# A softmax total moved from VectorE to ScalarE in a top-p graph attention kernel

## The chip, the cores and the metric

The kernel runs on one core of a Trainium2 chip. A core has five engines with an instruction stream each: TensorE (PE, whose weight loads the profile lists apart as PEld), VectorE (DVE), ScalarE (ACT), GpSimd (POOL) and SyncE (SP, which here only starts transfers). Each engine carries out its own instructions strictly in order, and the engines wait for each other through semaphores. The metric is the device time in microseconds (us) of one execution.

## The reference: what is computed

There are 3327 nodes with 256 features each. Layer 0 is a sparse graph attention with a gated update and two layer norms. Layer 1 makes two steps of a top-p ("nucleus") attention beside a propagation over the graph, then two layer norms. The change lies in layer 1, in its second step (n = 1):

```python
for n in range(STEPS):                       # STEPS = 2
    A = _top_p_attention(Xa, W1, W2, W3)     # 3327 x 3327, row-stochastic
    Xf = R @ Xf
    Xa = A @ Xa
    Z = Z + Xf @ U1[n].T + Xa @ U2[n].T

def _top_p_attention(X, W1, W2, W3):
    logits = (X @ W1.T @ W2.T) @ (X @ W3.T).T
    probs = softmax(logits)
    # keep the largest of each row until their sum reaches TOP_P = 0.9, drop the rest
    keep_sorted = cs - sp < TOP_P            # cs: running sum of the sorted sp
    A = probs * mask
    return A / max(A.sum(-1), 1e-12)
```

So each row of exponentials needs its total: 0.9 of the total is the mark at which the kept set ends.

## The kernel before, in words

The rows of the attention are cut into NT = 26 tiles of 128 rows (the last has 127). Layer 0 and step 0 of layer 1 take the first 900 us of the execution and are not touched. Step 1 is the class `Layer1`, method `run`, from its second `with` on. The order of the instructions on PE, ACT, DVE and POOL is written out by hand there: no scheduler moves them. The loop runs over tiles i, and each pass is one call of `product(i, slots)`: PE turns the 26 column blocks of the masked exponentials of tile i in seven groups of four (`turn`, L2052, with ACT copying each turned group out of PSUM, L2054) and multiplies them with the features (`times`, L2068). Two groups are turned ahead before the first product, and behind every group of products the functions that hang in that group's slot are issued. They belong to later tiles, so that four tiles are in work at once:

- tile i+3: its logits on PE (`chunk`, L1779), copied to SBUF by ACT (L1782), in slots 0 to 3;
- tile i+2: its candidates, the eight largest of each of 32 column groups, on DVE (`eights`, L1795) and minus the row's largest (`highest`, L1870) in slot 1; the exponentials of the candidates (`exp_candidates`, L1890) and of the first half of the row (`exp`, L1878) in slot 3, of the second half in slot 4. These are ACT's. Each half writes the sum of its own 1664 or 1663 exponentials into one column of a small tile `sums`; the trace shows this as an ACTIVATION_READ_ACCUMULATOR behind each half;
- tile i+1: `list_1` on DVE, issued ahead of slot 0: it takes the candidates' exponentials, tries four cut values (L1904, four passes with a sum each), makes `thr2` = 2 x 0.9 x (sum of the two halves) (L1907), compares the four sums with it (L1909), and sorts what is left; then in slot 1 `list_2` finds the smallest kept exponential, and in slot 3 `mask` (L1982, L1948) writes the masked row, which the next pass turns;
- tile i-1 and older: the layer norms, on ACT and POOL (`sums`, L2031 to L2043).

`thr2` is column 2 of a tile of four columns called `pay` (L1869), which has four buffers. Later readers of `thr2` are `settle` (L1829, DVE), `one_over` (L1958, POOL) and the transfer `put_aside_2` (L2140, POOL), which writes `pay` away for rows that the fast path cannot finish. Those rows are treated in a tail ("hard" rows, L2147 to L2313) behind the last tile; some of that work, L2207 and L2225 on ACT, lies between the last eight tiles.

At the start of a pass ACT's order is: second half's exponentials of tile i+1 (as counted from the new i) and their read-out (L1878), `h` of the tile just multiplied (`scaled`, L2076), and then the copy of the first turned group (L2054), for which PE waits before its first product. The prediction calls this place the handover.

Of the kernel before, what the change touches and what calls it, by code (L numbers as in the profile page):

```python
# [11 lines left out]
AF = mybir.ActivationFunctionType  # L12
ALU = mybir.AluOpType
# [13 lines left out]
TOP_P = 0.9  # L27
# [1221 lines left out]
class Layer1:  # L1249
# [91 lines left out]
    def parts_0(self, t):  # L1341
# [136 lines left out]
        def exp(k):  # L1478
# [3 lines left out]
            nc.scalar.activation(signs[:r, on], l[:r, on], AF.Exp, bias=v.nmax[:r], accum_out=v.sums[:r, k : k + 1])  # L1482

        parts["exp0"], parts["exp1"] = lambda: exp(0), lambda: exp(1)

        @part
# [387 lines left out]
    def exp(self, i, h):  # L1874

        v = self.items[i]
        on = slice(h * HALF, min(N, (h + 1) * HALF))
        self.nc.scalar.activation(  # L1878
            v.p[: v.r, on], v.l[: v.r, on], AF.Exp, bias=v.nmax[: v.r], accum_out=v.sums[: v.r, h : h + 1]
        )  # L1880

    def exp_candidates(self, i):

        v = self.items[i]
        width = -(-N // GROUP[v.n]) * 8
        if i == NT:
            v.ec = self.work.tile([P, 2 * D], F32, tag="xt", name=f"ec{v.tag}", bufs=3)[:, :width]
        else:
            v.ec = self.work.tile([P, width], F32, tag="xtq", name=f"ec{v.tag}")
        self.nc.scalar.activation(v.ec[: v.r], v.cand[: v.r], AF.Exp, bias=v.nmax[: v.r])  # L1890

    def list_1(self, i):

        nc, v = self.nc, self.items[i]
        r, tag, ec = v.r, v.tag, v.ec
        by_rank = ec[:r].rearrange("p (g e) -> p e g", e=8)
        first, end = TRIED
        tried = end - first
        high = self.small("high", f"high{tag}", tried)
        nc.vector.tensor_reduce(high[:r], by_rank[:, first:end, :], AX.X, ALU.max)  # L1900
        v.last = self.last_eights(ec, r, tag)
        above = self.small("upto", f"above{tag}", tried)
        for j in range(tried):
            nc.vector.scalar_tensor_tensor(  # L1904
                v.cand[:r], ec[:r], high[:r, j : j + 1], ec[:r], ALU.is_ge, ALU.mult, accum_out=above[:r, j : j + 1]
            )
        nc.vector.tensor_scalar(v.thr2[:r], v.sums[:r, 0:1], v.sums[:r, 1:2], 2.0 * TOP_P, ALU.add, ALU.mult)  # L1907
        over = self.small("at", f"over{tag}", tried)
        nc.vector.tensor_scalar(over[:r], above[:r], 2.0, v.thr2[:r], ALU.mult, ALU.is_ge)  # L1909
        v.e = self.work.tile([P, LIST[1] + 1], F32, tag="e", name=f"e{tag}")  # L1910
        v.lst = v.e[:, 1:]
        skip = self.small("u", f"skip{tag}")
        nc.vector.scalar_tensor_tensor(high[:r], over[:r], 2.0, high[:r], ALU.mult, ALU.max)
        nc.vector.tensor_reduce(skip[:r], high[:r], AX.X, ALU.min)
        nc.vector.scalar_tensor_tensor(v.cand[:r], ec[:r], skip[:r], ec[:r], ALU.is_lt, ALU.mult)
        nc.vector.scalar_tensor_tensor(above[:r], over[:r], 0.5, above[:r], ALU.is_lt, ALU.mult)
        nc.vector.tensor_reduce(v.e[:r, 0:1], above[:r], AX.X, ALU.max)
        for _ in self.sort(v.cand, r, LIST[1], tag, v.lst):
            pass
# [733 lines left out]
```

## Time and profile before

| what | value |
|---|---|
| median of 3 runs (lowest, highest) | 1627.8 us (1625.9, 1630.64) |
| profiled execution: its own time, its span | 1629.77 us, 1628.0 us |
| TensorE clock granted, mean over the span | 0.93 |
| busy over the span: PE, DVE, ACT, POOL | 87%, 84%, 68%, 64% |
| stage 0 to 880 us: layer 0 and step 0 | PE 780.6, DVE 700.9, ACT 644.5, POOL 517.2 us busy |
| stage 920 to 1440 us: most of step 1's tiles | PE 500.0, DVE 495.2, ACT 356.6, POOL 418.5 us busy |
| stage 1480 to 1628 us: the tail with the hard rows | PE 66.1, DVE 111.9, ACT 54.7, POOL 60.5 us busy |

How to read it: the time is that of a separate counter, the span is what the instructions of the profile cover; the two differ by 1.8 us. In a row of the timeline the first number is the start in us from the span's start, the second the duration, then engine, line, operation, what is written and read, and in brackets the idle time before and who ended it. Several neighbouring instructions of one line are merged (x8); fp32 matmuls appear as two passes each. A busy engine is not by that the one that sets the time: that is read from who waits for whom in the stage in question. The transposes' "weights" are the masked row, so that PE cannot begin them before DVE has masked it.

### The profile page before, as it was taken

How to read it: one execution, taken by the hardware profiler on the slowest of the kernel's cores; microseconds unless marked ns; L12 is line 12 of the kernel's file. 1: busy time of each engine (PE TensorE's matmuls, PEld its weight loads, DVE VectorE, ACT ScalarE, POOL GpSimd, SP SyncE). 2: the span in 40 equal slices, each digit the busy share in tenths (PEclk: the TensorE clock that was granted, in tenths of full speed). 3: DMA queues.
4: the chain of work that ended last, by engine and by line, in shares of the span. 5: the costliest groups of instructions: out<-in, count | busy, mean ns of one | idle time of the engine just before them, and what ended most of it. 6: DMA issues, size and time to landing. Idle time of an engine off the chain costs nothing. (4 is left out here: it accounts for less than half of the span.)

```text
span 1628.0 us, 27192 instructions
## 1 busy us (share of the span) xinstructions
PE 1414.7 (87%) x7743; PEld 967.2 (59%) x7743; DVE 1372.0 (84%) x4921; ACT 1103.1 (68%) x2690; POOL 1036.4 (64%) x1484
## 2 busy tenths in 40 slices
PE   4899999986899899998988899999999999988334
PEld 3756666554455555555555477777777666666233
DVE  5799999537888888888874899999999998987984
ACT  4478888755688878888774567676666777773730
POOL 0366666514566766767654378888888878877440
PEclk7599999996799999999999799999999999999667
DMA  8978776314334444444443112222222222121000
GB/s 261 329 248 261 261 256 178 83 40 123 95 113 117 124 127 111 123 118 128 124 113 85 38 49 68 72 72 75 66 75 58 75 62 75 54 59 33 26 13 5
DMA packets 101636, 178.80 MB, mean 110 GB/s; under 512 B 25975, under 2 KB 64118, under 8 KB 101478
## 3 DMA queue, kind: packets, MB, share of 16 engines
q0 software_dynamic: 26288, 73.75, 17.5%
q1 hardware_dynamic: 61818, 93.49, 17.4%
q10 hardware_dynamic: 13372, 9.76, 1.9%
q8 instruction: 63, 1.03, 0.3%
q14 instruction: 95, 0.78, 0.2%
HBM read 139.92 MB, written 37.07 MB: 109 GB/s over the span
## 5 line engine op out<-in xcount | busy, mean ns | idle before, releaser
L2068 PE MATMUL pav<-xu,at 128*128 128x256 f32 (+2 forms) x1352 | 339.1, 396 | 20.4 <-ACT at L2054 20.4
L2068 PEld LDWEIGHTS pav<-xu,at 128*128 128x128 f32 (+2 forms) x1352 | 249.2, 194 | 113.4 <-issue 44.6
L1782 ACT COPY array<-pl 128x416 f32<-128x416 f32 (+3 forms) x402 | 184.3, 512 | 125.9 <-PE pl L1779 125.6
L1795 DVE MAX8 cand<-array 128x8 f32<-128x104 f32 (+5 forms) x1233 | 260.5, 288 | 7.0 <-ACT array L1782 6.8
L1779 PE MATMUL pl<-kT,qT 64*128 64x416 f32 (+3 forms) x804 | 205.7, 570 | 9.2 <-ACT array L1782 8.0
L2054 ACT COPY at<-pt 128x512 f32<-128x512 f32 (+2 forms) x182 | 95.4, 539 | 106.3 <-PE pt L2052 106.0
L677 POOL DMA_INDIRECT g<-x_rows,edge x130 | 136.9, 1053 | 45.0 <-issue 30.3
L677 POOL DMA_INDIRECT g<-whx,edge x130 | 134.9, 1038 | 46.9 <-issue 37.2
L677 POOL DMA_INDIRECT g<-y_rows,edge x130 | 136.6, 1051 | 36.9 <-issue 35.6
L1608 POOL DMA_INDIRECT g<-x1k,uidx x130 | 136.6, 1051 | 36.8 <-issue 25.7
L945 DVE FIND_INDEX8 at<-ones,array 128x8 uint32<-128x840 f32 (+1 forms) x104 | 105.9, 1027 | 0.0
L1779 PEld LDWEIGHTS pl<-kT,qT 64*128 64x128 f32 (+1 forms) x804 | 66.8, 188 | 65.8 <-issue 44.3
L1705 POOL TENSOR_TENSOR x<-x,c 128x256 f32<-128x256 f32 (+1 forms) x26 | 17.7, 684 | 73.5 <-ACT c L1700 73.5
L1062 PE MATMUL acc<-g,m 128*128 128x258 f32 (+1 forms) x260 | 62.7, 388 | 0.0
L2011 PE MATMUL pxf<-g,m 128*128 128x256 f32 (+1 forms) x260 | 62.4, 387 | 0.0
L1062 PEld LDWEIGHTS acc<-g,m 128*128 128x128 f32 (+1 forms) x260 | 50.5, 195 | 18.4 <-issue 7.4
L1666 PE MATMUL pav<-g,w 128*128 128x257 f32 (+1 forms) x260 | 60.9, 380 | 0.0
L2085 POOL TENSOR_TENSOR h<-h 128x256 f32<-128x256 f32 (+1 forms) x26 | 58.7, 2257 | 2.0
L1904 DVE SCALAR_TENSOR_TENSOR cand<-ec,high 128x256 f32<-128x256 f32 (+1 forms) x104 | 57.0, 548 | 2.8
L1089 PE MATMUL prz<-wih,hT 128*128 128x512 f32 (+1 forms) x104 | 52.1, 625 | 3.5 <-ACT hT L1082 1.6
L701 PE MATMUL pq<-xtq,wkqk 128*128 128x128 f32 (+1 forms) x208 | 35.5, 295 | 21.5 <-ACT xtq L693 15.4
L701 PEld LDWEIGHTS pq<-xtq,wkqk 128*128 128x128 f32 x208 | 29.9, 195 | 39.3 <-ACT xtq L693 38.1
(578 smaller groups left out, 3809.9 us busy)
## 6 DMA issues: line engine op xcount, KB each, us to landing
array<-in_adj_dram SPq DMA_DIRECT2D x25, 1248.0 KB
array<-in_adj_dram SPq DMA_DIRECT2D x25, 415.5 KB
members<-m SPq DMA_DIRECT2D x26, 320.0 KB
m<-members SPq DMA_DIRECT2D x26, 320.0 KB
x_rows<-x ACTq DMA_DIRECT2D x25, 128.0 KB
x1k<-x ACTq DMA_DIRECT2D x25, 128.0 KB
xb_rows<-xb SPq DMA_DIRECT2D x25, 128.0 KB
y_rows<-y SPq DMA_DIRECT2D x25, 128.0 KB
```

Of the source, the lines that this page charges most:

```text
L677: self.nc.gpsimd.indirect_dma_start(out=dst[:, b, :], out_offset=None, in_=table[:, :], in_offset=bass.IndirectOffsetOnAxis(ap=self.edge[: ...
L701: nc.tensor.matmul(pq[:, :r], self.wkqk[:, c, h * DA : h * DA + P], xt[:, c, :r], start=(c == 0), stop=(c == DC - 1))
L945: nc.vector.max_index(at[:r, g, :], self.ones8[:r], ad[:r, g, :])
L1062: nc.tensor.matmul(acc[:r, : self.WH], m[:, :r], g[:, k, :], start=(k == 0), stop=(k == EB - 1))
L1608: nc.gpsimd.indirect_dma_start(out=v.g2[:, b, :], out_offset=None, in_=sh.x1k[:, :], in_offset=bass.IndirectOffsetOnAxis(ap=v.idx[:, b : b ...
L1666: nc.tensor.matmul(v.acc[:r, : D + 1], v.w[:, b, :r], v.g2[:, b, : D + 1], start=(b == 0), stop=(b == UB - 1))
L1779: nc.tensor.matmul(pl[:r, :w], q[on], self.sh.kT[on, n, s : s + w], start=True, stop=True)
L1782: nc.scalar.copy(l[:r, h * HALF + s : h * HALF + s + w], pl[:r, :w])
L1795: self.nc.vector.max(cand[:r, g * 8 : g * 8 + 8], src[:r, g * group : min(N, (g + 1) * group)])
L2011: nc.tensor.matmul(acc[:r, :D], v.m[:, b, :r], v.g[:, b, :], start=(b == 0), stop=False)
L2054: nc.scalar.copy(at[:, :full, :r], pt[:, :full, :r])
L2068: nc.tensor.matmul(v.acc[: v.r, :D], at[:k, j - 4 * g, : v.r], V[:k, j, :], start=(j == 0), stop=(j == NT - 1))
```

## The change

`thr2` is no longer made on DVE in `list_1`. ACT makes it right behind the second half's exponentials, with two instructions on 128x1 operands: the first half's sum is scaled in place by 2 x 0.9, and the second half's sum is scaled by the same factor and added to it, the first serving as per-partition bias. `list_1` loses one instruction.

```diff
@@ def exp(self, i, h):
         self.nc.scalar.activation(
             v.p[: v.r, on], v.l[: v.r, on], AF.Exp, bias=v.nmax[: v.r], accum_out=v.sums[: v.r, h : h + 1]
         )
+        if h:
+            a, b = v.sums[: v.r, 0:1], v.sums[: v.r, 1:2]
+            self.nc.scalar.activation(a, a, AF.Copy, scale=2.0 * TOP_P)
+            self.nc.scalar.activation(v.thr2[: v.r], b, AF.Identity, bias=a, scale=2.0 * TOP_P)
@@ def list_1(self, i):
-        nc.vector.tensor_scalar(v.thr2[:r], v.sums[:r, 0:1], v.sums[:r, 1:2], 2.0 * TOP_P, ALU.add, ALU.mult)
         over = self.small("at", f"over{tag}", tried)
         nc.vector.tensor_scalar(over[:r], above[:r], 2.0, v.thr2[:r], ALU.mult, ALU.is_ge)
```

In the built program this adds 52 instructions to ACT (two for each of 26 tiles), each waiting for the ACT instruction before it, and takes 26 from DVE. The order on PE, POOL and SP is the same as before, and ACT and DVE keep the order of all else. The comparison L1909 waits for ACT's second new instruction, where L1907 used to wait for the read-out. In 22 of the 26 tiles the second new instruction also waits for the transfer that last read its buffer of `pay`, four tiles earlier. Behind the change, lines of the file shift by 4 (up to L1907 of before) or 3.

## The prediction

> **What bounds the kernel now.** I read the stage that holds the change first: the busy time by stretch, then who waits for whom in it.
>
> ```profile
> core 0: us, PE busy (x) PEld busy (x) DVE busy (x) ACT busy (x) POOL busy (x), PEclk, DMA share, GB/s
> 920.00:1440.00 520.00, 499.95 (x2493) 370.24 (x2492) 495.21 (x1640) 356.57 (x810) 418.54 (x694) 0.99 0.23 67
> ```
> ```profile
> PE pav L2068 <- ACT at L2054: 13.1, 22, 1.9
> ...
> DVE pay L1907 <- ACT array L1878: 0.8, 1, 0.8
> ```
>
> PE (96%) and DVE (95%) are both nearly full, ACT is at 69%. That would favour taking work from DVE. But PE's largest wait is for ACT: 22 times, once a tile, for the copy at the handover (columns: us in total, times, longest). DVE waits almost not at all. So the handovers have to be read one by one in the timeline. There are three kinds. The first, at 966 us:
>
> ```profile
> 966.07 1.07 PE L2052 MATMUL pt<-ident,array 128*128 128x128 f32 x8
> 967.44 1.78 PE L2068 MATMUL pav<-xu,at 128*128 128x256 f32 x7 [0.29 <-ACT at L2054]
> ...
> 966.23 0.21 ACT L1878 ACTIVATION_READ_ACCUMULATOR p<-array,pay 128x1 f32 x1
> 966.33 0.49 ACT L2076 ACTIVATE h<-pav,rA 128x256 f32<-128x256 f32 x1
> 966.80 1.07 ACT L2054 COPY at<-pt 128x512 f32<-128x512 f32 x2
> ```
>
> The copy begins 0.73 us after the transposes; PE's first product always follows the copy's start by 0.64 to 0.66. The copy stands 0.47 behind L2076; where nothing holds it, that distance is 0.36 (third kind, below). So ACT has 0.11 us to spare. Here DVE is not in the way (the mask ended at 964.91): PE runs at its own pace, from 944.37 over 966.07 to 987.77, 21.70 a tile. The second kind, from 1009.65 to 1206.85, ten handovers:
>
> ```profile
> 1075.18 0.08 DVE L1948 DVE_READ_ACCUMULATOR p<-p,t 128x1 f32 x1
> ...
> 1075.41 1.06 PE L2052 MATMUL pt<-ident,p 128*128 128x128 f32 x8
> ...
> 1075.32 0.21 ACT L1878 ACTIVATION_READ_ACCUMULATOR array<-array,pay 128x1 f32 x1
> 1075.41 0.49 ACT L2076 ACTIVATE h<-pav,rA 128x256 f32<-128x256 f32 x1
> 1076.13 1.07 ACT L2054 COPY at<-pt 128x512 f32<-128x512 f32 x2 [0.23 <-PE pt L2052]
> ```
>
> Each time the transposes start 0.15 to 0.16 after the mask's end: DVE sets the pace, (1206.85 - 1009.65) / 9 = 21.91 a tile, only 0.21 above PE's own. ACT's spare is 0.28 to 0.36. The third kind, 1345.95 to 1415.74, where hard-row work (L2225) lies on ACT too:
>
> ```profile
> 1371.14 0.48 ACT L2076 ACTIVATE h<-pav,rA 128x256 f32<-128x256 f32 x1
> 1371.49 1.09 ACT L2054 COPY at<-pt 128x512 f32<-128x512 f32 x2
> ...
> 1372.15 1.99 PE L2068 MATMUL pav<-xu,at 128*128 128x256 f32 x8 [1.86 <-ACT at L2054]
> ```
>
> ACT never stops before the copy and PE stands still for 1.86 us: no spare at all.
>
> **What is removed.** One L1907 in each of 26 tiles on DVE.
>
> ```profile
> 1076.58 0.08 DVE L1904 DVE_READ_ACCUMULATOR cand<-ec,high 128x1 f32 x1
> 1076.70 0.49 DVE L1904 SCALAR_TENSOR_TENSOR cand<-ec,high 128x256 f32<-128x256 f32 x1
> ...
> 1077.64 0.08 DVE L1904 DVE_READ_ACCUMULATOR cand<-ec,high 128x1 f32 x1
> 1077.64 0.21 DVE L1907 TENSOR_SCALAR pay<-sums 128x1 f32<-128x1 f32 x1
> 1077.88 0.23 DVE L1909 TENSOR_SCALAR over<-above,pay 128x4 f32<-128x4 f32 x1
> ```
>
> L1907 overlaps the read-out. L1909 needs the read-out itself, and what depends on one starts 0.12 behind its start (1076.58 to 1076.70): it moves from 1077.88 to 1077.76. So DVE gains 0.12 a tile, not 0.24: its pace where it leads would be 21.79. Where L1909 already follows ACT, nothing is gained.
>
> **What is added.** Two dependent ACT instructions, between the read-out (start A) and L2076. The nearest rows:
>
> ```profile
> L2037 ACT ACTIVATE junk2bt<-h,minbt 128x256 f32<-128x256 f32 x21 | 10.9, 521 | 0.0
> ...
> L2031 ACT ACTIVATE junkbt<-h 128x256 f32<-128x256 f32 x21 | 9.0, 430 | 0.0
> ...
> L2033 ACT ACTIVATE minat<-sat 128x1 f32<-128x1 f32 x22 | 4.5, 203 | 0.7
> ```
>
> (Columns: busy us, mean ns, idle before.) L2033 is the very Copy (128x1, 203 ns, behind a read-out). The Identity has a pointer bias besides: L2037 has one and L2031 none, 521 - 430 = 91 ns, so about 295 ns (an estimate). L2033 starts 0.22 behind the read-out's start (1060.36 to 1060.58). The Copy then starts at A + 0.22, the Identity a Copy and a gap of 0.03 later at A + 0.455, and L2076, which need not wait for it, about 0.2 on at A + 0.655, against A + 0.09 now: ACT's handover is 0.56 us later.
>
> Here a rule of the Trainium skill decides (ScalarE: Activation LUTs, section "What ACT_TABLE_LOAD costs"): an ACTIVATE has some 186 ns of fixed cost, each pointer operand adds about 93, and instructions back to back overlap by about 93. The 91 ns agree. By the overlap the two would cost 0.09 + 0.19 = 0.28, all but hidden by the spare of the second kind, and the total would be about +1 us. But the overlap is that of independent instructions (read-out to L2076: 0.09); the dependent row shows 0.22. I take 0.56; 0.28 is the lower end, and 0.7 the upper if either semaphore costs a little more. No new function is used (Exp, Copy and Identity alternate now), so I add no table load. The wait for the transfer out of `pay` costs nothing: L1870 on DVE wrote that buffer after the same landing, and the exponentials read it.
>
> Queued behind on ACT: L2076, whose reader on POOL (L2077, at 1081.23) has over 5 us; and the copy L2054, for which PE waits, with all its later work in order behind. From the first product on PE has no idle time in a tile of the first two kinds, so a delay there is not made up within the tile.
>
> On the DVE side, where L1909 waits for ACT it moves from read-out end + 0.28 to about + 0.58: +0.30. Six tiles wait so now (906, 1324, 1347, 1370, 1443, 1467 us); elsewhere the slack is up to 2.2 us. DVE then still masks more than 1 us ahead of PE.
>
> **The sum.**
> - Start: the first pair of exponentials (906 us) stands before copies on the chain to the first handover: +0.5.
> - 944 to 1207: the delay is 0.56 - 0.11 = 0.45, PE's pace 22.15, above DVE's 21.79. Twelve tiles: 12 x 22.15 = 265.8 against 262.5: +3.3. The gain on DVE is lost in this, since PE now sets the pace.
> - 1229 and 1251: 0.45 each; 1274: 0.2, as L2076 waits for POOL there anyway; 1299 and 1324: 0.35 each (spare 0.21): +1.8.
> - Given back: PE's wait of 0.8 for POOL's flag at 1212 and some 0.9 for a gather at 1281 (0.4 idle, 0.5 stretched) lie on DVE's and POOL's chain, which is not delayed as much: -1.7.
> - 1346 to 1416: four with no spare, +2.2; 1466: +0.6. At 1442 ACT waits 2 us for POOL: 0.
> - The last tile's L1909 lies on the chain into the tail: +0.3.
>
> Together +7.0 us, on a span of 1628.0. The profiled execution (1629.77) lies 2 us above the median; on the median this is **1634.8 us**.
>
> **The rivals.**
> 1. *Hidden or given back.* ACT is idle a third of the stage; the read-outs may cost only the 0.28 above, or the first half's loss may be returned at 1268 to 1299, where the chain runs through DVE (L1948) and POOL and not through PE's pace: then only 1299 onward counts, 0.7 + 2.2 + 0.6 + 0.3 = 3.8, or +1 by the overlap. Time 1627 to 1632. For it: that chain is in the trace. Against: DVE itself becomes tied to ACT's new end there (slack 1.4 to 1.7 before a delay of 3).
> 2. *Faster: DVE is the bound throughout.* The skill's page on trace analysis (Perfetto Trace Analysis, "Optimizing Scalar/DVE Operations") says that with a saturated DVE it can pay to move operations to ScalarE. If the full start-to-start 0.24 counts in all 26 tiles, -6.2: 1621.6. It decides if ACT's spare at the handovers is at least the delay added; the rows show 0 to 0.36, against 0.56. Besides, only ten handovers follow the mask.
> 3. *Worse: every handover pays in full.* 24 x 0.56 = 13.4, with nothing given back: 1641, if the spare of 0.11 isn't there and POOL's two-input operations fall worse behind the masks (L2105 took 3.58 us at 1270 instead of 0.2, behind L1948).
>
> **How the numbers follow.** The forecast (+5 to +9) has 0.53, rival 1 0.26, rival 2 0.05, rival 3 (over +9) 0.16. 0.3% is 4.9 us, about what a measurement can tell here from no change: slower 0.69, same 0.26, faster 0.05. The range leaves out rival 2, the lower half of rival 1 and the worst of rival 3: 1628.5 to 1641.5.
>
> **What would show it.** Right: L2076 starts 0.5 to 0.6 behind its read-out; the starts of the transposes between 944 and 1207 lie 22.1 apart and no longer 0.16 behind the mask; PE's wait for L2054 grows from 13 to about 22 us; L1909 starts 0.12 behind its last read-out in quiet tiles. Wrong: dependent ACT instructions that overlap after all, or a period still at 21.8, with transposes at the mask's end.

## The result and the profile after

Over six runs of each on one chip the kernel after takes 1641.89 us in the median (1638.81 to 1645.7), the kernel before 1626.78 us (1623.74 to 1630.64). The ratio is 1.0084 with a 95% interval of 1.0066 to 1.0102: the change makes the kernel about 14 us slower. The forecast was slower by 7 us. The profiled execution of after takes 1640.78 us, with a span of 1638.9 us against 1628.0 us before. So this pair of executions differs by 10.9 us only: the profiled one of before lies 3 us above its median, that of after 1 us below. The stages below account for these 10.9 us; the rest of the 14 was not traced.

The same views as in the prediction, now of the kernel after. First the waits between 920 and 1440 us (us in total, times, longest):

```profile
PE pav L2071 <- ACT at L2057: 23.9, 25, 2.7
...
DVE high L1904 <- ACT ec L1894: 11.1, 4, 3.6
ACT h L2046 <- POOL mvat L2044: 6.2, 4, 2.7
...
DVE over L1912 <- ACT pay L1884: 4.7, 6, 1.0
```

and two of these waits before:

```profile
DVE high L1900 <- ACT ec L1890: 4.2, 2, 2.4
ACT h L2043 <- POOL mvat L2041: 3.2, 2, 2.6
```

PE's wait at the handover has grown from 13.1 to 23.9 us, and its longest from 1.9 to 2.7. Two waits that were there before come four times instead of twice: DVE's for the candidates' exponentials of ACT (11.1 us instead of 4.2), and ACT's for a result of the layer norm from POOL (6.2 instead of 3.2). The timeline at a quiet handover of after:

```profile
1101.39 1.07 PE L2055 MATMUL pt<-ident,array 128*128 128x128 f32 x8
1101.55 0.21 ACT L1878 ACTIVATION_READ_ACCUMULATOR p<-array,pay 128x1 f32 x1
1101.64 0.21 ACT L1883 ACTIVATE sums<-sums 128x1 f32<-128x1 f32 x1
1101.88 0.29 ACT L1884 ACTIVATE pay<-sums 128x1 f32<-128x1 f32 x1
1102.09 0.46 ACT L2079 ACTIVATE h<-pav,rA 128x256 f32<-128x256 f32 x1
1102.44 1.06 ACT L2057 COPY at<-pt 128x512 f32<-128x512 f32 x2
1103.07 0.70 PE L2071 MATMUL pav<-xu,at 128*128 128x256 f32 x2 [0.61 <-ACT at L2057]
```

L2079 (L2076 before) starts 0.54 behind the read-out where it started 0.09 behind, and the copy 1.05 behind the transposes where it was 0.72. PE idles 0.61 instead of 0.29. The transposes lie 22.02 us apart from 946.14 to 1211.47 us, with one exception. They no longer follow the mask at 0.15: the mask now ends 0.7 to 1.9 us ahead of them. PE sets the pace through ACT. On DVE, a little later:

```profile
1103.18 0.08 DVE L1908 DVE_READ_ACCUMULATOR cand<-ec,high 128x1 f32 x1
1103.37 0.23 DVE L1912 TENSOR_SCALAR over<-above,pay 128x4 f32<-128x4 f32 x1
```

The comparison starts 0.19 behind the last read-out (0.24 before), so DVE has gained 0.05 us a tile. And a handover of the third kind, where the hard rows' pass lies on ACT:

```profile
1352.18 1.07 PE L2055 MATMUL pt<-ident,p 128*128 128x128 f32 x8
1352.34 0.21 ACT L1878 ACTIVATION_READ_ACCUMULATOR array<-array,pay 128x1 f32 x1
1352.43 0.21 ACT L1883 ACTIVATE sums<-sums 128x1 f32<-128x1 f32 x1
1352.68 0.29 ACT L1884 ACTIVATE pay<-sums 128x1 f32<-128x1 f32 x1
1352.88 1.67 ACT L2228 ACTIVATE xh<-x,minush_0.0625_17398 128x1664 bf16<-128x1664 f32 x1
...
1355.52 2.62 PE L2071 MATMUL pav<-xu,at 128*128 128x256 f32 x7 [2.28 <-ACT at L2057]
```

PE's pause is 2.28 instead of 1.86: again 0.42 more. At the next three handovers it is 2.66, as in this row:

```profile
1382.37 2.17 PE L2071 MATMUL pav<-xu,at 128*128 128x256 f32 x7 [2.66 <-ACT at L2057]
```

The tiles that begin at 1352, 1379, 1405 and 1431 us take 26.46, 26.63, 25.46 and 26.64 us, where they took 23.26 three times before and 26.22 once. This is more than the added pause. The starts of the transposes in both profiled executions give the difference by stage:

| stage (on before's clock) | forecast | measured |
|---|---|---|
| up to the first handover at 944 us | +0.5 | +1.8, of which 1.4 lie before step 1's first exponential |
| 944 to 1207 | +3.3 | +2.9 |
| 1207 to 1346 | +1.8 - 1.7 | +1.6 |
| 1346 to 1442, four tiles with L2225 | +2.2 | +9.2 |
| 1442 to 1466 | 0 | -1.7 |
| 1466 to the end | +0.6 + 0.3 | -2.8 |
| sum | +7.0 | +10.9 |

So the question for the experiments is the fourth row: why an added pause, 0.42 at first, costs more than 2 us a tile on average.

**A window of the clock.** In the four tiles of after the granted clock falls to half for one stretch of 3.41 us behind three of the pauses. All such stretches of one execution lie on one fixed grid of 3.413 us. These are the stretches of that grid around the handovers of after; the columns are duration, then busy time of PE, PEld, DVE, ACT and POOL, then the granted clock, DMA share and GB/s:

```profile
core 0: us, PE busy (x) PEld busy (x) DVE busy (x) ACT busy (x) POOL busy (x), PEclk, DMA share, GB/s
1352.89:1356.31 3.42, 1.14 (x8) 0.83 (x7) 3.06 (x12) 3.07 (x6) 2.73 (x3) 1.00 0.14 39
1356.31:1359.72 3.41, 3.41 (x12) 2.51 (x12) 3.13 (x13) 0.26 (x1) 2.91 (x8) 0.50 0.27 77
...
1404.09:1407.50 3.41, 2.10 (x14) 1.66 (x14) 2.43 (x10) 3.38 (x7) 2.92 (x3) 1.00 0.13 39
1407.50:1410.92 3.42, 1.92 (x9) 1.66 (x10) 3.18 (x13) 1.94 (x5) 2.81 (x8) 1.00 0.29 77
```

and of before:

```profile
1391.98:1395.39 3.41, 1.57 (x13) 1.17 (x11) 3.20 (x13) 3.41 (x7) 3.07 (x5) 1.00 0.00 0
1395.39:1398.80 3.41, 3.39 (x17) 2.37 (x18) 3.17 (x13) 1.07 (x3) 2.67 (x4) 1.00 0.14 39
1415.87:1419.28 3.41, 1.55 (x12) 1.26 (x11) 3.16 (x14) 3.24 (x7) 2.91 (x3) 1.00 0.01 0
1419.28:1422.69 3.41, 3.41 (x13) 2.44 (x11) 3.13 (x11) 0.00 (x0) 2.75 (x7) 0.50 0.30 77
```

In after PE was idle for 2.28 of the window at 1352.89 (1.14 busy), and the next one runs at 0.50. The pause at 1405 is as long or longer, but an edge of the grid cuts it (1.3 and 1.5 us idle): no fall. In before two windows differ by 0.02 us of busy time, and only the one with 1.55 busy is followed by a slow one. Its pause of 1.86 us was just at the mark. I counted this for step 1 of all 13 profiles taken here: of the windows at full clock, none of those in which PE was idle for less than 0.54 of the window was followed by a slow window, all 49 with more than 0.58 idle were, and of nine between them four were.

**A block behind the mask.** The second thing in these tiles is on POOL; the timeline of after:

```profile
1368.07 0.20 ACT L2040 ACTIVATION_READ_ACCUMULATOR junk2at<-h,minat 128x1 f32 x1
...
1368.78 3.69 DVE L1951 SCALAR_TENSOR_TENSOR array<-array,t 128x3327 f32<-128x3327 f32 x1
1368.80 0.20 POOL L2044 TENSOR_TENSOR mvbt<-minbt,mvbt 128x1 f32<-128x1 f32 x1
1369.08 3.44 POOL L2042 TENSOR_SCALAR mvat<-sqat 128x1 f32<-128x1 f32 x1
...
1373.45 0.60 ACT L2046 ACTIVATE h<-h,mvat 128x256 f32<-128x256 f32 x1 [2.42 <-POOL mvat L2044]
```

The same place before:

```profile
1361.71 0.19 POOL L2041 TENSOR_TENSOR mvat<-minat,mvat 128x1 f32<-128x1 f32 x1
...
1362.85 3.68 DVE L1948 SCALAR_TENSOR_TENSOR array<-array,t 128x3327 f32<-128x3327 f32 x1
1362.96 3.73 POOL L1845 TENSOR_SCALAR flag<-many,short 128x1 f32<-128x1 f32 x1
```

In each of these four tiles of after one POOL instruction that starts inside the mask on DVE takes 3.2 to 3.7 us, and ends with the mask. (L2044 at 1368.80, 0.02 us behind the mask's start, is not held.) The Trainium skill has this behaviour (SBUF — State Buffer, "SBUF: two separate sides": a DVE operation with two SBUF inputs and a POOL operation that reads SBUF exclude each other for the whole instruction), and the rows agree: 3.44 us for what takes 0.20 elsewhere. Before, L1845 was hit in this tile, for which nobody waits. In after it is L2042, in the chain of the layer norm, for whose result ACT waits 2.42 us in order. The norm's first POOL instruction starts 15.7 us behind the tile's transposes here and 13.7 before; the mask starts at 16.6 and 16.9. So 2.0 us of delay, the 0.42 of the pause and the rest from the slow window, carry the norm into the mask.

The kernel before has the same pair once, in its tile of 26.22 us: behind the slow window at 1419 us the mask holds L2041 of the norm for 3.61 us, and ACT waits 2.58 us.

### The profile page after: what moved, and what is told of

The parts are those of the page before. It is cut to its first block, busy times and chain, and to the rows that moved or that the text cites. A ratio compares the mean times of both kernels' runs of the same rounds, so it can differ in the third digit from the quotient of the medians.

```text
span 1638.9 us, 27167 instructions
## 1 busy us (share of the span) xinstructions
PE 1418.5 (87%) x7743; PEld 967.6 (59%) x7743; DVE 1371.6 (84%) x4895; ACT 1111.5 (68%) x2742; POOL 1034.7 (63%) x1484
## 5 line engine op out<-in xcount | busy, mean ns | idle before, releaser
L1908 DVE SCALAR_TENSOR_TENSOR cand<-ec,high 128x256 f32<-128x256 f32 (+1 forms) x104 | 64.0, 616 | 2.8
L2014 PEld LDWEIGHTS pxf<-g,m 128*128 128x128 f32 (+1 forms) x260 | 48.3, 194 | 8.5 <-DMA g<-y_rows,edge 1.5
```

The lines of the kernel that those rows point to most:

```text
L2014: nc.tensor.matmul(acc[:r, :D], v.m[:, b, :r], v.g[:, b, :], start=(b == 0), stop=False)
```

## The experiments

Several groups of runs were made on other chips. On two of them the kernel before takes about 1744 and 1748 us, the extra lying ahead of step 1. Therefore I give beside each ratio the stretch of step 1 in the profiled execution, from the start of its first exponentials (L1878) to the start of its last: 562.1 us before and 574.3 us after.

**1. ACT's two instructions alone.** DVE keeps its own total; the results of the two on ACT are used by nobody.

```diff
+        if h:
+            dead = self.small("dead", f"dead{v.tag}", 2)
+            self.nc.scalar.activation(dead[: v.r, 0:1], v.sums[: v.r, 0:1], AF.Copy, scale=2.0 * TOP_P)
+            self.nc.scalar.activation(
+                dead[: v.r, 1:2], v.sums[: v.r, 1:2], AF.Identity, bias=dead[: v.r, 0:1], scale=2.0 * TOP_P
+            )
```

> VectorE makes thr2 as before the change; ScalarE makes the two small instructions as well, and nobody reads what they give. Theory A (ScalarE is late at the handover, TensorE pays): as slow as the change, 12 to 16 us above before, transposes 22.0 us apart in the quiet tiles. Theory B (VectorE waits for a thr2 that comes later from ScalarE, and is late with the masks): within 2 us of before.

Measured: 1757.19 us, ratio 1.0071 (1.0047 to 1.0094), stretch 574.4. Its waits over the same 520 us of the stage:

```profile
PE pav L2074 <- ACT at L2060: 23.8, 24, 2.7
DVE high L1906 <- ACT ec L1896: 11.5, 4, 4.2
```

The transposes are 22.03 apart, and four of the last tiles take 25.4 to 27.1. Ratio and stretch are close to those of after. So the loss is all in ACT's two instructions. That DVE must now wait for ACT, and what DVE gains, can be left out of the account.

**2 and 3. The change in the first twenty tiles only, and in the last six only.** Condition on `i` at the two places of the diff:

```diff
+        if h and i < NT + 20:      # 3: i >= NT + 20
...
+        if i >= NT + 20:           # 3: i < NT + 20
             nc.vector.tensor_scalar(v.thr2[:r], ...)
```

> The change in the first 20 tiles of step 1 only; the six tiles whose handovers hold the coarse passes of the hard rows are as before. Theory A without amplification: 20 x 0.45 less the spare, about +5 us over before, of which +4.5 are there by the start of the hard tiles. Theory C (what was lost beyond +5 comes from the six last tiles alone: the clock falls in TensorE's longer pause, and GpSimd falls behind VectorE's mask): the same +4 to +6, and the last tiles 23.3 us apart as before. If the loss in the last tiles comes from where the first tiles put the engines against each other, +10 or more.

> The change in the last six tiles only. Theory A without amplification: 6 x 0.45, +2 to +3 us over before. Theory C (the pause at the handover grows from 1.86 to 2.3 us, TensorE's clock halves behind it, GpSimd's small norm work then falls behind VectorE's mask): +6 to +10, with several drops of the granted clock between 1340 and 1450 us and tiles of 25 to 27 us.

The first twenty: ratio 1.0031 (1.0018 to 1.0044), stretch 566.2, that is +4.1. The transposes are 22.01 apart. Of the four tiles with the hard rows' pass, three take 23.26 us as before; the fourth takes 24.94, with a fall of the clock but no block on the norm (26.22 with both before). From the first handover to the first of these four the stage is 3.9 us longer, where the forecast's sum has 3.4. This part of the sum stands. The last six: ratio 1.0020 (1.0003 to 1.0036), single runs from 1739.1 to 1757.5 us, stretch 561.2. The profiled execution has the longer pause, but no fall of the clock and no block on the norm in four tiles of 23.67 us (23.26 + 0.41). That is far from the 9 us that these tiles cost in after, and the falls that the second theory expected did not come. Even together the two halves cost less than the whole change, some 9 us of time by their ratios. The grid windows of the last-six kernel at the first of these handovers:

```profile
1461.15:1464.56 3.41, 2.23 (x16) 1.74 (x14) 2.06 (x8) 3.38 (x5) 3.08 (x5) 1.00 0.26 82
1464.56:1467.98 3.42, 2.33 (x12) 1.94 (x12) 3.18 (x13) 1.52 (x5) 2.72 (x4) 1.00 0.27 77
```

The same pause of 2.27 us is cut in two by the grid, 1.2 and 1.1 us. So the longer pause alone costs 0.41 a tile (0.56 was forecast); what more it costs depends on where it falls on the grid. That this makes the spread of the runs is likely, but it wasn't shown.

**4. The total on ACT, but behind the first two copies of the pass,** in tiles 1 to 19 of step 1; the first and the last six keep it on DVE.

```diff
+        for f in pre:      # in product(), behind turn(i, 0) and turn(i, 1)
+            f()
...
+                    if i + 1 < NT + 20:
+                        pre.append(lambda i=i: self.total(i + 1))
+                    pre.append(lambda i=i: self.list_1(i + 1))
```

> In the tiles 1 to 19 of step 1 ScalarE makes thr2, but behind the two copies of the next tile's first turned groups instead of in front of them; the other tiles as before. VectorE saves its instruction there as with the change, and thr2 comes about 2.3 us after the transposes, when VectorE wants it. Theory A: the handover is as before, so the time is within 2 us of before, or up to 2 us below it, with transposes 21.7 to 21.9 us apart. Theory B: VectorE gets thr2 even later than with the change, so at least as slow as the change in these tiles, +4 us or more.

Measured: ratio 1.0027 (1.0011 to 1.0044), single runs 1737.1 to 1758.6; stretch 560.1. The handovers are as before (PE idle 0.29), and the transposes 21.86 to 21.95 apart, each 0.15 behind the mask. DVE's 0.05 a tile isn't seen in the pace. The 2 us that the stage is shorter than before are not the total's doing: they are less than what its last tile with L2225 saves (23.25 us, without a fall, against 26.22). The whole time, 4 us above before in the median, misses the forecast of at most 2; why is open.

**5. The kernel after once more, with two variations, on one chip.**

> The kernel after, once more, beside the two that vary it. Each theory: step 1's stretch from the first to the last first-half exponential (L1878) about 576 us, 12 above before; pairs of transposes 22.0 apart between 946 and 1211 us on the first chip's clock. If the cost of the last tiles depends on how the engines happen to stand (as the change confined to the last tiles suggested), the tile periods there may differ from the 26.5, 26.6 and 25.5 us of the first profile, and be anything from 23.7 to 27.

After: 1764.47 us against 1748.31, ratio 1.0098 (1.0070 to 1.0126), stretch 576.3. The four tiles take 26.4, 26.9, 25.5 and 26.9 us, with pauses of 2.27 and then three times 2.65 or 2.66, and the falls of the clock lie in the same tiles as in the first profile of after. So here the large cost comes back. Behind the last handover (1597 us) it takes 165.0 us, where the first profile of after took 159.0 and before 161.8: the tail varies by more than the -2.8 in the table, which can't be put down to the change.

The first variation keeps PE busy in the pause, with products that nobody reads, in the PSUM tile that the real products then use:

```diff
+        if i >= NT + 19:           # in product(), behind turn(i, 0) and turn(i, 1)
+            self.keep_busy(i)
...
+        v.acc = self.pac.tile([P, 512], F32, tag="av", name=f"pav{v.tag}")
+        for _ in range(4):
+            self.nc.tensor.matmul(v.acc[:, :D], self.ident, self.xu[:, 0, :], start=True, stop=True)
```

> The kernel after, with four matmuls without use on PE between the transposes and the first products of the last seven tiles, so that PE does not stand still there. Theory 'clock': the pauses of 2.3 to 2.7 us at these handovers bring the half-speed window of 3.4 us behind them, which lengthens the products by some 1 to 1.7 us a tile; with PE kept busy no window comes, and the tiles of 26.5 us fall to 24 to 25: 4 to 7 us less than after. Rival 'block': the long POOL operation behind DVE's mask does it alone, and a busy PE changes nothing: 0 to +1 us against after (the four matmuls may push the first product by up to 0.3 us a tile).

1753.52 us, ratio to before 1.0032 (1.0019 to 1.0045), so 11 us less than after; stretch 566.6, 9.6 less. The grid windows of its first handover of this kind:

```profile
1469.57:1472.98 3.41, 2.87 (x15) 2.23 (x14) 3.15 (x12) 2.97 (x5) 2.62 (x3) 1.00 0.14 39
1472.98:1476.39 3.41, 3.41 (x19) 2.36 (x18) 3.13 (x14) 1.51 (x4) 3.01 (x8) 1.00 0.32 77
```

PE no longer stops there, and the clock stays at 1.00. All four tiles take 23.67, POOL's block falls on L1842, L2108 and L1844, and L2042 to L2044 are free. ACT's copy comes 2.72 us behind the transposes each time, as at the first of these handovers in after. So the clock comes first: work without use on PE takes the fall away, and the block on the norm goes with it. That is why more was saved than the 4 to 7 us expected. The pause of 2.66 goes too: it is found only in tiles behind one with the norm blocked (in both profiles of after and in experiment 1), so the block lengthens the next pause as well, by 0.38.

The second variation moves DVE's mask later instead:

```diff
+        if NT + 19 <= i < STEPS * NT - 1:
+            spare = self.small("spare", f"spare{tag}", 8)
+            nc.vector.max(spare[:r], v.p[:r, :1400])
         self.drop(v.p[:r], v.d, v.t, r, 0, tag, v.gone)
```

> The kernel after, with a DVE pass of about 1.5 us (the maximum of 1400 columns, not used) ahead of the mask of the last tiles, so that POOL's short chain of L2042 and L2044 is over before the mask (L1951) starts. Theory 'block': POOL's L2042 no longer takes 3.4 us, ACT gets L2044's result in time, PE and DVE do not wait in the last products: about 4 to 5 us less than after although DVE has 9 us more to do. Rival 'DVE': the longer chain on DVE comes through, since the mask is what the next transposes wait for: up to 1.4 us a tile, +5 to +9 us against after.

1759.22 us, ratio to before 1.0071 (1.0045 to 1.0096), 5 us less than after, with intervals that overlap, so the time alone doesn't show it; stretch 569.7, 6.6 less, although DVE does some 9 us more. Windows, then timeline:

```profile
1494.20:1497.61 3.41, 1.38 (x12) 1.00 (x11) 2.33 (x11) 3.38 (x8) 2.85 (x5) 1.00 0.15 45
1497.61:1501.02 3.41, 3.16 (x8) 2.54 (x9) 3.13 (x11) 0.68 (x2) 2.87 (x7) 0.50 0.24 59
```
```profile
1486.10 0.20 POOL L2045 TENSOR_SCALAR mvat<-sqat 128x1 f32<-128x1 f32 x1
...
1488.29 3.71 DVE L1954 SCALAR_TENSOR_TENSOR array<-array,t 128x3327 f32<-128x3327 f32 x1
1488.52 3.98 POOL L2022 TENSOR_TENSOR h<-h,x 128x256 f32<-128x256 f32 x1
```

The clock still falls in two tiles, but the norm's chain is over when the mask starts. Those two take 50.53 us together, 25.27 each against 23.68 for the next, which has no fall. That separates the terms, in single tiles: a fall alone costs 1.6 us (1.7 in the fourth tile of experiment 2), the block without a fall 1.8 (the tile at 1405 us of after, 25.46 against 23.67, with the 0.38 of longer pause in it), both together 2.8 to 3.0. The fourth row of the table is then made up of four longer pauses, 1.6; three tiles with both and one with the block, 10.5; less the 3.0 that before pays for its own tile with both. That is 9.1 of 9.2.

**6. Room at the handover.** The kernel before with the hard rows' pass of ACT (L2225) moved out of slot 5 and behind the first two copies of the next pass:

```diff
-                    for g in (0, 2, 5) if i + 3 < total else (0, 1, 2, 5, 6):
+                    for g in (0, 2) if i + 3 < total else (0, 1, 2, 5, 6):
                         slot(g, go_on, g == 2)
+                    if closing > 5 and i + 2 < total:
+                        pre.append(go_on)
```

> The kernel before (the total on DVE), with the pass of ScalarE for the hard rows (L2225) in the last tiles issued behind the first two copies of the next pass instead of ahead of the handover. My theory says that the last tiles are set by what ACT has to do ahead of the copy for PE: PE's waits of 1.86 us in four tiles go, and with them a half-speed window or two: 6 to 9 us less than before. Rival: ACT is late elsewhere then, since the third and fourth groups' copies stand behind the pass: 0 to 3 us less.

1740.45 us against 1748.31 on the same chip, ratio 0.9956 (0.9944 to 0.9968); stretch 555.0. In four of the first five of the last tiles PE's idle time at the handover is back to 0.29 (1.02 in the other), with L2225 behind the copies:

```profile
1490.36 0.92 PE L2068 MATMUL pav<-xu,at 128*128 128x256 f32 x3 [0.29 <-ACT at L2054]
```

This beats both kernels. The same move in the kernel after, the total behind the copies beside the move, and the busy PE in the kernel before were run together, on a chip where before takes 1628.22 us:

> The kernel after (total made at the handover in all tiles) with ScalarE's pass for the hard rows (L2225) moved behind the first two copies of the next pass. If the large cost in the last tiles comes from a pause that is already long and that the change lengthens past the point where the clock falls, it is gone with the pass out of the way, and the change costs only what it costs in quiet tiles: step 1's stretch about 555 + 3 to 5 = 558 to 560 us, that is below the 562 of before. Rival: the change costs the last tiles its 9 us whatever ACT's room is there: about 567 us.

> The kernel before with two edits: ScalarE's pass for the hard rows (L2225) behind the first two copies of the next pass in the last tiles, and the total made by ScalarE, but behind those copies too, in the first twenty tiles. Theory: the total costs nothing there, and brings nothing either, since PE's own pace of 21.7 a tile lies only 0.2 below DVE's: the same as the pass moved alone, 0 to -1 us (step 1's stretch 554 to 555 us, against 562 before). Rival: DVE's 0.06 to 0.12 us a tile come through in the ten tiles that follow the mask: another 0.6 to 1.2 us less, with transposes 21.8 apart.

> The kernel before with four matmuls without use on PE between the transposes and the first products of the last seven tiles. Theory: before, PE's pauses of 1.86 us lie just under the length that brings a half-speed window, and only one of the four tiles has one; so keeping PE busy saves little where it saved the kernel after some 10 us: 0 to 3 us less than before. Rival: it saves as much here, 7 to 10 us, and then the clock isn't what tells the two kernels apart.

The kernel after with the move: 1624.58 us, ratio 0.9984 (0.9973 to 0.9995), stretch 557.5. A handover of it in the last tiles:

```profile
1374.07 0.21 ACT L1883 ACTIVATE sums<-sums 128x1 f32<-128x1 f32 x1
1374.32 0.29 ACT L1884 ACTIVATE pay<-sums 128x1 f32<-128x1 f32 x1
1374.52 0.46 ACT L2079 ACTIVATE h<-pav,rA 128x256 f32<-128x256 f32 x1
1374.87 1.06 ACT L2057 COPY at<-pt 128x512 f32<-128x512 f32 x2
1375.50 1.35 PE L2071 MATMUL pav<-xu,at 128*128 128x256 f32 x5 [0.61 <-ACT at L2057]
1375.82 1.71 ACT L2228 ACTIVATE xh<-x,minush_0.0625_17398 128x1663 bf16<-128x1663 f32 x1
```

The change is all there, but the pauses are 0.5 to 0.9 and far from the mark, no window of these four tiles is slow, and they take 22.0 to 22.4. The stretch is 2.5 us over that of the move alone (555.0, on another chip), where the change costs 12.3 without the move; by the ratios to before, 0.9984 against 0.9956, it is some 4.6 us of the whole time against 14 to 17. The total behind the copies in tiles 1 to 19, with the move: 1623.97 us, ratio 0.9976 (0.9964 to 0.9988), stretch 556.6. That is not better than the move alone (0.9956 and 555.0, on another chip), and the rival's pace of 21.8 isn't there: the quiet tiles are 21.9 apart. So no gain of ScalarE's total is seen even where it stands out of the handover's way. The busy PE in the kernel before: ratio 0.9984 (0.9975 to 0.9994), stretch 558.7, that is 3.3 less, where the same edit took 9.6 from after. The median is 2.9 us lower (0 to 3 were expected). Before has one fall of the clock in the four tiles, after three; that one tile goes from 26.22 to 23.26.

## Why the prediction was right, and where its size was off

Direction and place were right: PE waits for ACT's copy at the handover, and DVE's relief is worth nothing. The size was half of what came, 7 us of some 14. The median of after, 1641.9 us, lies just above the upper end of the range, 1641.5, and that it is so near is not to the credit of the sum: its term for the last tiles missed what sets their cost. Step by step:

- *What is removed*: DVE was to gain 0.12 a tile. It gained 0.05; the comparison follows the last read-out by 0.19 and not 0.12. Nothing hangs on it, and experiments 1 and 4 show that the pace doesn't contain it.
- *What is added*: 0.56 at the handover was 0.45. The first instruction scales the *first* half's sum, which has been there for long, so it starts 0.09 behind the second read-out, overlapping it; I had charged the dependent 0.22. Lengths (0.21, estimate 0.295 against 0.29) and the 0.2 to L2076 were right. The rule of the Trainium skill on overlapping instructions (ScalarE: Activation LUTs, "What ACT_TABLE_LOAD costs") fits the first of the two; the second, which needs the first's result, starts 0.24 behind the first's start, and by the rule alone (0.28, an estimate) the loss would have been too small.
- *944 to 1207*: the delay was 0.33 beyond the spare instead of 0.45, since 0.45 less a spare of 0.12 remains; PE's pace 22.02, not 22.15. That gives 1.7 us over these tiles, and 1.1 more came in one tile, where PE waited 0.86 for a gather: POOL's transfer `left_over` ahead of it had waited 2.62. The sum of 2.9 is near the forecast's 3.3 in part by luck, since this term was not in it. It belongs to the change, though: the tile takes 22.8 to 23.2 us in all the other profiles with ACT's two instructions in the early tiles. The trace puts the wait of `left_over` down to DVE (L1917); why it came just there was not followed.
- *Given back, -1.7*: it didn't come. PE's wait for POOL's flag grew from 0.8 to 1.1 instead of going, and the tile with it takes 23.22 (22.52 before). Before, the mask ahead of this handover held L2085 of POOL, the last instruction ahead of the transfers (at 1203.29, for 3.99 us); in after it holds L1962 (at 1206.87, for 4.01 us), with L2086 and L2088 still to do behind it, and the flag comes 5.9 us behind the transposes instead of 5.2. The gather's tile, at 1274, gave back 0.2 instead of 0.7. The forecast also left the handover at 1207 itself out of its sum. The row came to +1.6 instead of +0.1.
- *1346 to 1416, four with no spare, +2.2*: this is the step that failed. I carried the delay of 0.56 through each tile one for one. The delay itself was near (0.42), and experiment 3 shows an execution where it is all. But the pause which it lengthens was already 1.86 us, 0.545 of a clock window; at 2.28 it is 0.67 and gives a slow window wherever the grid doesn't cut it. The slow window moves the norm's chain into the mask's block, and the block makes the next pause longer, 2.66. The four tiles cost 9.2 instead of 2.2. Experiment 5 shows the order of causes. I had the pause of 1.86 us in a fence and the granted clock in another, and read neither against the other; before's own slow window at 1419 us was in the trace.
- *From 1442 to the end*: +0.9 forecast, -4.5 measured in this pair of executions. Part of it is before's own long stop and slow windows at 1443, which after doesn't have in that form; the tail varies by 6 us between two profiles of after. It was not traced further.
- *Rivals*: rival 3 has the right size, 13 to 14 us, and half of its mechanism (POOL falling worse behind the masks; but not POOL's two-input operations alone, for L2105 and L2042 have one input), but not its main term: 24 handovers paying in full would put 0.56 on each quiet tile, and these pay 0.1 to 0.3 over the pace of before. Rival 2 fell: the mark it names, spare against delay, decides against it. Rival 1 fell with the given-back part.

The Trainium skill's rule about the clock (TensorE: Matmul & The Clock Gate, "Part 1: The HAM clock gate") has the free-running window of 3413 ns, and the traces agree to the nanosecond's rounding. It says that the clock falls after an idle window, and under "HAM oscillation" it warns of pauses above some 3.4 us. By that, pauses of 2.3 us would be harmless: +0.4 a tile, as I forecast without it. The runs show falls from 0.54 of a window idle, so the measurement decides.

## What to carry to other kernels

Before adding work ahead of a place where PE waits, look at how long PE's pause there already is, and not only at whether there is spare: here a pause of about 1.9 us stood just at the point where 0.4 us more brings half the clock for 3.4 us. Moving the large operation (L2225, 1.7 us) out from in front of the handover was worth more than any small one put in or taken out, and made the small one cheap. And in a fixed order of engines, a delay decides which instruction is caught by an exclusion such as the one between DVE's mask and POOL; whether anybody waits for that instruction decides its price.

## What was not expected of the hardware

- The half-speed window comes from idle time within one window of a fixed grid of 3.413 us, with a mark between 0.54 and 0.58 of it, in all 13 profiles. Two pauses of the same length (2.27 us, experiments 3 and 6) had different fates by where the grid cut them.
- Four matmuls without use a tile, put into pauses of 2.3 to 2.7 us, made the kernel after 11 us faster (1753.5 against 1764.5).
- A 128x1 instruction of ACT behind another on which it depends starts 0.22 to 0.26 us behind its start (0.24 in the median of the 26 tiles of after); one that doesn't depend starts 0.09 behind.
- The mask on DVE (3.7 to 4.2 us) held exactly one POOL instruction in each of the four last tiles with L2225 of all 13 profiles, for 3.1 to 4.1 us, also such with one input of 128x1.
